# Layer 1 self attention of a Perceiver block: eight steps put in another order

## The chip, the cores and the metric

The kernel runs on one core of one Trainium2 chip. The metric is the time of one execution on the device in microseconds (us), as the median of several runs. Lower is better. All arithmetic is float32.

## What is computed

The reference is a two-layer Perceiver on 64 sequences of 32 tokens with 256 features. Each layer adds a cross attention, a self attention and a feed-forward part to `x`. The change lies in the last two parts of layer 1. In short, with `ln` the layer norm:

```python
# self attention: 16 heads of 16 features, 4 groups of keys and values
q = einsum('bse,hed->bhsd', ln(x), Wq) + bq
k, v = repeat(kg, 4), repeat(vg, 4)          # kg, vg: 4 groups, from ln(x)
scores = einsum('bhqd,bhkd->bhqk', q, k) / sqrt(d)      # causal mask
x = x + concat_heads(softmax(scores) @ v)
# experts: each token goes to the one expert with the highest router value
route = sigmoid(ln(x) @ router_w)            # 8 experts
e, p = argmax(route), max(route)
x = x + p * ((silu(ln(x) @ gate_w[e]) * (ln(x) @ up_w[e])) @ down_w[e])
```

## The kernel before

The 2048 tokens are 16 tiles of 128 rows (four sequences each), called `xs[0]` to `xs[15]`; they stay on the chip. Four tiles make a group, since a projection takes 512 columns at once. TensorE (PE), VectorE (DVE) and ScalarE (ACT) run exactly in the order in which the program is written: these stages are inside `manual_schedule` for the three. GpSimd (POOL) and the DMA queue of SyncE (SP) are ordered by the framework's planner.

**The attention loop.** `for t in range(NT - 3)` at the end of the kernel is a pipeline written out by hand. In turn t, PE computes the scores of tile t+1 (`score`), the result of tile t-1 (`gather`), the values of tile t+1 (`values`), and the turn of tile t's probabilities (`heads_on_partitions`, L286, copied by ACT in L288). Around them lie the pieces of other work:

- `softmax_rows` reads the scores on DVE (L268, L277), and POOL subtracts the maximum (L278). `power(t + 1)` takes the exponential on ACT (L2120).
- `place_values` copies the values of tile t+1 out of the PSUM bank "v" into a block form: one quarter on DVE (L2144), three on ACT (L2146). There is one bank "v", so `values` of the next tile waits until all four copies are done.
- `gather` ends with a reciprocal and a product on DVE (L2161, L2163) and an addition into `xs[t-1]` on POOL (L2166).
- `group(g, part)` prepares the next group of four tiles: part 0 turns the normalised tiles (`transposed_part`, PE L261, ACT L262) in two halves, both through the bank "mm"; parts 1 and 2 are the projections (L1476), copied by ACT.
- `bias` and `norm` (L1459, L205) prepare later groups; `load_piece` starts the loads of expert weights on SP.

**The router**, within the same loop. For a set of tiles (`ROUTED`: 0 to 3, then pairs): `route_stats` takes mean and variance on DVE (L179, L180), and after the set's last tile `route_scale` makes the norm's scale on POOL (L164 to L1840, eight small operations for a pair). `route_norm` applies it on ACT (L1849), `route_turn` turns it (PE L1865, ACT L1870), `route` multiplies with the router's weights (PE L1879) and takes an exponential on ACT (L1888). `choose_expert` finds the best expert on DVE (L1894 to L1904; POOL stores the weight in L1905). `places` ranks the tokens within each expert by matmuls with `oh` and `cum` (L1918, L1921; DVE L1925 to L1930). `send` writes each token's row to its place in a sorted array in memory by an indirect DMA on POOL (L1938). `heat` issues matmuls whose result nobody uses (L1909).

**After the loop** the last three tiles and the first expert tiles are written out turn by turn. The expert part works on 20 tiles of 128 sorted rows: `load_rows` (SP, L2217; it waits for all sends so far), `rows_norm` (DVE L2247), `rows_turn` (PE L2263, ACT L2265), `gate` and `up` (PE, L2307), `hidden_of` (ACT L2337, DVE L2338, L2339), `turn_hidden` (PE L2346, ACT L2351), `down` (PE L2307, DVE L2362, and an indirect DMA to the output on POOL, L2365). Tiles 0 to 2 may start once the first 10 token tiles are sent, tiles 3 and 4 after 12, the rest after all 16 (`give_count`, `give_table`). The banks "o", "mm", "PT" and "v" of PSUM are each there once; two uses of one bank follow each other.

Of the kernel before, what the change touches and what calls it, by code (L numbers as in the profile page):

```python
# [15 lines left out]
NT = B * S // P  # L16
# [23 lines left out]
def bc(ap, axis, n):  # L40

    shape = list(ap.shape)
    shape.insert(axis, n)
    return ap.unsqueeze(axis).to_broadcast(shape)
# [3 lines left out]
def perceiver_kernel(ctx: ExitStack, tc: tile.TileContext, a: dict, out: bass.AP):  # L48
# [209 lines left out]
    def transposed_part(xn, xT, ps, k, name, tag="mm"):  # L258
        tp = ps.tile([P, 512], F32, tag=tag, name=f"tp_{name}_{k}")
        for i in range(4):  # L260
            nc.tensor.transpose(tp[:, i * P : (i + 1) * P], xn[i][:, k * P : (k + 1) * P], ident)  # L261
        nc.scalar.copy(xT[:, k, :], tp)  # L262
# [18 lines left out]
    def heads_on_partitions(s, ps, t, work, name):  # L281

        pt = ps.tile([P, 512], F32, tag="PT", name=f"ptp_{name}{t}")
        sf = s.rearrange("p h k -> p (h k)")
        for c in range(4):
            nc.tensor.transpose(pt[:, c * P : (c + 1) * P], sf[:, c * P : (c + 1) * P], ident)  # L286
        pT = work.tile([P, 4, P], F32, tag="pT", name=f"pT_{name}{t}")
        nc.scalar.copy(pT.rearrange("p c q -> p (c q)"), pt)  # L288
        return pT
# [110 lines left out]
    with tc.tile_pool(name="wA", bufs=2) as work, tc.tile_pool(  # L400
# [77 lines left out]
        def power(t):  # L478
            nc.scalar.activation(sc[t], sc[t], AF.Exp)
# [39 lines left out]
        def gather(t):  # L519
            pT, vd = turned.pop(t), vals.pop(t)  # L520
            o_ps = ps1.tile([P, KC, P], F32, tag="o", name=f"oa{t}")
            for j in range(4):
                for c in range(4):
                    p0 = 64 * (c % 2)
                    nc.tensor.matmul(
                        o_ps[p0 : p0 + 64, c // 2, j * S : (j + 1) * S],
                        vd[:, j, c].rearrange("p h d -> p (h d)"),
                        pT[:, c, j * S : (j + 1) * S],
                        start=True,
                        stop=True,  # L530
                    )
            oT = ctxo[t] = work.tile([P, KC, P], F32, tag="oT", name=f"oTa{t}")
            nc.scalar.copy(oT, o_ps)


            if 2 <= t < 10:
                z, h4 = divmod(t - 2, 4)
                if z == 0:
                    dst = b_q[:, h4 // 2, (h4 % 2) * 1024 : (h4 % 2) * 1024 + 1024]
                    src = a["b_wq"].rearrange("(k p) o -> p k o", p=P)[  # L540
                        :, h4 // 2, (h4 % 2) * 1024 : (h4 % 2) * 1024 + 1024
                    ]
                    nc.gpsimd.tensor_copy(dst[:, 0:1], oT[:, 0, 0:1])
                else:
                    dst = b_o[:, 4 * h4 : 4 * h4 + 4, :]
                    src = a["b_wo"].rearrange("(h p) o -> p h o", p=P)[:, 4 * h4 : 4 * h4 + 4, :]
                    nc.gpsimd.tensor_copy(dst[:, 0, 0:1], oT[:, 0, 0:1])
                nc.sync.dma_start(dst, src)
# [338 lines left out]
    with tc.tile_pool(name="wB", bufs=2) as work, tc.tile_pool(  # L887
# [228 lines left out]
        ff, late = {}, []  # L1116
# [705 lines left out]
    def route_stats(t):  # L1822
        ts = next(ts for ts in ROUTED if t in ts)
        if t == ts[0]:
            rows[ts] = sm(f"lnf_{t}", [P, 4, 2])
        stats(rows[ts][:, t - ts[0], :], xs[t], f"f{t}")
        if t == ts[-1]:
            route_scale(ts)
# [43 lines left out]
    def route(ts, ps, tag):  # L1872

        n_, t0 = len(ts), ts[0]
        xT = rows.pop(ts)[1]
        l_ps = ps.tile([P, n_, NE], F32, tag=tag, name=f"lpf{t0}")
        for i in range(n_):
            for k in range(KC):
                nc.tensor.matmul(  # L1879
                    l_ps[:, i, :],  # L1880
                    xT[:, k, i * P : (i + 1) * P],
                    f_r[:, k, :],
                    start=(k == 0),
                    stop=(k == KC - 1),
                )
        rt = sm(f"rtf_{t0}", [P, n_, NE])

        nc.scalar.activation(rt, l_ps, AF.Exp, scale=-1.0)  # L1888
        return lambda: choose_expert(ts, rt)

    def choose_expert(ts, rt):

        n_, t0 = len(ts), ts[0]
        nc.vector.tensor_scalar_add(rt, rt, 1.0)  # L1894
        nc.vector.reciprocal(rt, rt)
        mx = sm(f"mxf_{t0}", [P, n_])
        nc.vector.tensor_reduce(mx, rt, AX.X, ALU.max)
        nc.vector.tensor_tensor(rt, rt, bc(mx, 2, NE), ALU.is_equal)
        nc.vector.tensor_tensor(rt, rt, bc(desc[:, 0:NE], 1, n_), ALU.mult)
        m2 = sm(f"m2f_{t0}", [P, n_])  # L1900
        nc.vector.tensor_reduce(m2, rt, AX.X, ALU.max)
        nc.vector.tensor_tensor(oh[:, t0 : t0 + n_, :], rt, bc(m2, 2, NE), ALU.is_equal)
        for i, t in enumerate(ts):
            nc.vector.tensor_add(cum[:, t + 1, :], cum[:, t, :], oh[:, t, :])  # L1904
            nc.gpsimd.tensor_scalar(xf[t][:, D + 1 : D + 2], mx[:, i : i + 1], 0.5, None, ALU.mult)  # L1905
# [172 lines left out]
    with tc.tile_pool(name="wE", bufs=2) as work, tc.tile_pool(  # L2078
# [14 lines left out]
        def group(g, part):  # L2093


            if g >= NG or part == 3:
                return []
            if part == 0:
                e_group_start(g)
                return [  # L2100
                    lambda k=k: transposed_part(lat[g], feats[g][2], ps2, k, f"e{g}")
                    for k in range(KC)
                ]
            return [lambda o=o: e_features(g, part, o, ps2) for o in range(KC)]
# [32 lines left out]
        def place_values(t, v_ps, rs_=range(4)):  # L2137

            for r in rs_:
                rs = slice(32 * r, 32 * r + 32)  # L2140
                dst = vd[t % 3][rs].rearrange("p j c h d -> p (j c) h d")[:, :, r, :NH]
                src = v_ps[rs].rearrange("p j (c d) -> p (j c) d", c=4)
                if r == 0:
                    nc.vector.tensor_copy(dst, src)  # L2144
                else:
                    nc.scalar.copy(dst, src)  # L2146
# [31 lines left out]
        def choose_now():  # L2178
            for fn in chosen:
                fn()  # L2180
            chosen.clear()
# [215 lines left out]
        for t in range(NT - 3):  # L2397


            at_ = t + (t > 2)  # L2400
            parts = group(at_ // 4 + 1, at_ % 4) if t > 1 else []
            parts += router_parts(t)
            if t > 0:
                score(t + 1, idle=int(t > 10))
            if t < 12:
                load_piece()
            if t in (6, 11):
                route_norm(steps_n[t], work)
            for t_ in sends.get(t, ())[:1]:
                send(t_)  # L2410
            for fn in parts[:1]:
                fn()
            if t > 0:
                gather(t - 1)
            if t < 12:
                load_piece()
            for t_ in sends.get(t, ())[1:]:
                send(t_)
            for fn in parts[1:2]:
                fn()  # L2420
            choose_now()
            if t in (8, 9):

                route_norm(steps_n[t], work)
            v_ps[t + 1] = values(t + 1)
            place_values(t + 1, v_ps[t + 1], (0,))
            for fn in parts[2:3]:
                fn()
            choose_now()
            turned[t] = heads_on_partitions(sc.pop(t), ps1, t, work, "e")  # L2430
            power(t + 1)
            late = t < NT - 5
            if not late:
                place_values(t + 1, v_ps.pop(t + 1), (1, 2, 3))
            for fn in parts[3:]:
                fn()
            if t in steps_n:
                route_turn(steps_n[t], work, ps2, ("o", "mm"))
            if late:
                place_values(t + 1, v_ps.pop(t + 1), (1, 2, 3))  # L2440
            norm((t + 1) // 4 + 2, (t + 1) % 4, "e", mvs, lat)
            if t % 4 in (0, 3) and 0 < (t + 1) // 4 < NG - 1:
                bias((t + 1) // 4 + 1, t % 4 == 0)
            if 0 < t:
                route_stats(t - 1)
            if 1 < t < 10:
                load_piece()
# [21 lines left out]
        route_stats(t - 1)  # L2469

        t = NT - 2
        chosen.append(route(p10, ps1, "mm"))
        norms_to(1)
        gather(t - 1)
        choose_now()
        give_done()
        norms_to(2)
# [46 lines left out]
        turn_rows_to(4, "mm")  # L2524
        turn_rows_to(5, "v")
        hidden_of(2)
        places(p14, ps1, "o")
        for t_ in p14:
            send(t_)
        give_count(NT, ps1, "PT")  # L2530
        down(1, "mm")
        turn_hidden(2, "v")
        give_table()
        loads_to(FIRST[2] + 4)
# [140 lines left out]
```

## Time and profile before

| what | value |
|---|---|
| median of 3 runs | 1144.27 us (1143.97 to 1146.88) |
| the profiled execution | 1134.37 us, of which 1132.3 us are the span from first to last instruction |
| PE busy | 1092.7 us (97% of the span) |
| DVE, ACT, POOL busy | 769.7, 572.8, 465.8 us (68%, 51%, 41%) |
| granted TensorE clock | 0.999 (mean) |
| attention of layer 1 | first scores at 899.2 us, last at 990.2 us |
| expert products | first at 997.4 us; from 1035.4 us on one tile takes 5.8 us of PE |

A busy share is a mean over the whole span: it tells which engine is short of time over all, not what a single wait costs. A timeline line gives start, duration, engine, source line, operation, output and inputs, count, and in brackets how long the engine was idle before it and what ended that idle time. In a table of waits the three numbers are the total in us, the number of times, and the longest. "issue" stands for idle time that no wait of the program explains.

### The profile page before, as it was taken

Reading aid. Unit: us, or ns where it says so; the run is one execution under the profiler, and the core shown is the slowest. Engines: PE = TensorE matmul, PEld = TensorE weight load, DVE = VectorE, ACT = ScalarE, POOL = GpSimd, SP = SyncE. Lnnn points to the kernel's source line nnn. Section 1 sums busy time; section 2 is a strip of 40 time slices with the busy share of each in tenths; the row PEclk is TensorE's granted clock in tenths of the full one; section 3 lists DMA queues with packets and bytes.
Section 4 is the critical chain, followed back from the end, with each engine's and each line's share of the span. In section 5 each row is a group of like instructions: output and inputs, shape, how many; then the busy total and the mean of one; then the engine's idle time right before and its main releaser. Section 6 shows DMA issues by size and latency. Waiting matters only on the chain. (4 is left out here: it accounts for less than half of the span.)

```text
span 1132.3 us, 26384 instructions
## 1 busy us (share of the span) xinstructions
PE 1092.7 (97%) x10024; PEld 779.8 (69%) x10024; DVE 769.7 (68%) x1804; ACT 572.8 (51%) x1436; POOL 465.8 (41%) x781
## 2 busy tenths in 40 slices
PE   8999999999999989999999999999999988889997
PEld 5667867777677646677776777777777656656653
DVE  6887167677988997764226787777878666775532
ACT  4446354455354465232237777777777456442221
POOL 2443438878678687510001121111222346742111
PEclk9999999999999999999999999999999999999999
DMA  6220143654444544690232121223230044312413
GB/s 155 65 91 22 33 127 116 175 160 121 127 128 130 176 136 143 215 251 19 76 75 32 29 57 30 75 57 85 57 84 20 1 118 130 107 40 71 157 42 118
DMA packets 98958, 109.05 MB, mean 96 GB/s; under 512 B 37208, under 2 KB 73433, under 8 KB 98610
## 3 DMA queue, kind: packets, MB, share of 16 engines
q1 hardware_dynamic: 96290, 102.92, 32.1%
q0 software_dynamic: 1728, 4.33, 1.1%
q8 instruction: 80, 1.31, 0.5%
q14 instruction: 44, 0.36, 0.1%
q10 hardware_dynamic: 816, 0.13, 0.1%
HBM read 76.36 MB, written 31.41 MB: 95 GB/s over the span
## 5 line engine op out<-in xcount | busy, mean ns | idle before, releaser
L1556 ACT ACTIVATE pp<-Sd,nm 128x256 f32<-128x256 f32 x256 | 119.6, 481 | 40.6 <-POOL nm L1553 40.6
L919 PEld LDWEIGHTS qb<-xT_b,b_q 128*128 128x128 f32 x512 | 94.7, 190 | 39.0 <-issue 19.0
L919 PE MATMUL qb<-xT_b,b_q 128*128 128x256 f32 x512 | 121.3, 385 | 0.0
L1553 POOL TENSOR_SCALAR nm<-nm 128x2 f32<-128x2 f32 x128 | 26.9, 210 | 219.1 <-DVE nm L1552 218.9
L1010 PE MATMUL yb<-b_o,oTb 128*128 128x256 f32 x512 | 113.5, 380 | 0.5 <-DVE oTb L1002 0.5
L1552 DVE TENSOR_REDUCE nm<-Sd 128x2 f32<-128x512 f32 x128 | 79.4, 682 | 49.1 <-PE Sd L1539 49.1
L1010 PEld LDWEIGHTS yb<-b_o,oTb 128*128 128x128 f32 x512 | 96.4, 190 | 14.4 <-issue 1.8
L1574 DVE TENSOR_TENSOR pp<-pp,rd 128x512 f32<-128x512 f32 x128 | 89.6, 700 | 4.4
L1590 ACT COPY pTd<-pt 128x512 f32<-128x512 f32 x128 | 68.8, 591 | 10.3 <-PE pt L1584 4.2
L927 ACT COPY qTb<-qb 128x512 f32<-128x512 f32 x64 | 37.4, 584 | 69.8 <-PE qb L919 65.8
L938 POOL TENSOR_TENSOR q2b<-qTb 128x512 f32<-128x512 f32 x64 | 64.7, 1041 | 14.6 <-ACT qTb L927 14.6
L1584 PE MATMUL pt<-cst,pp 128*128 128x128 f32 x512 | 67.8, 274 | 2.5 <-DVE pp L1574 1.3
L1584 PEld LDWEIGHTS pt<-cst,pp 128*128 128x128 f32 x512 | 59.1, 141 | 11.9 <-ACT ld L1564 2.1
L972 DVE RECIPROCAL rqb<-rqb 128x512 f32<-128x512 f32 x16 | 53.5, 3342 | 17.8 <-ACT rqb L967 17.8
L1343 PE MATMUL qd<-xT_d,d_m 128*128 128x256 f32 x256 | 62.6, 387 | 0.7 <-DVE rd L1573 0.3
L1631 PE MATMUL yd<-d_n,co 128*128 128x256 f32 x256 | 63.2, 391 | 0.0
L1565 POOL TENSOR_TENSOR sd<-sd,ld 128x2 f32<-128x2 f32 x128 | 26.3, 205 | 86.2 <-ACT ld L1564 86.2
L1539 PE MATMUL Sd<-ct,qTd 64*128 64x256 f32 x480 | 60.0, 388 | 0.0
L1605 PE MATMUL od<-pTd,na 128*64 128x256 f32 x480 | 58.4, 385 | 0.0
L773 PE MATMUL yc<-c,hc 128*128 128x256 f32 x256 | 58.4, 381 | 0.0
L1631 PEld LDWEIGHTS yd<-d_n,co 128*128 128x128 f32 x256 | 46.2, 189 | 16.7 <-DVE nm L1552 7.7
L986 DVE RECIPROCAL rdb<-denb 128x512 f32<-128x512 f32 x16 | 53.7, 3355 | 5.8 <-PE denb L984 5.6
(462 smaller groups left out, 2407.9 us busy)
## 6 DMA issues: line engine op xcount, KB each, us to landing
srt<-pad SPq DMA_DIRECT2D x17, 1040.0 KB
mb<-maskd SPq DMA_DIRECT2D x64, 128.0 KB
ct<-ctd SPq DMA_DIRECT2D x30, 257.0 KB
rct<-in_ctxT_dram SPq DMA_DIRECT2D x32, 128.5 KB
rrt<-in_ctxT_dram SPq DMA_DIRECT2D x64, 64.2 KB
ctd<-rct SPq DMA_DIRECT2D x32, 128.5 KB
nad<-rna SPq DMA_DIRECT2D x16, 256.0 KB
fg<-in_f_wg_dram SPq DMA_DIRECT2D x16, 256.0 KB
```

Source lines behind the costliest of these rows:

```text
L773: nc.tensor.matmul(y_ps, hs[f][:, i * P : (i + 1) * P], c_2[:, f, :], start=(f == 0), stop=(f == 7),)
L919: nc.tensor.matmul(q_ps[:, hh, :], b_q[:, k, h * P : (h + 1) * P], xT[:, k, c0 : c0 + 256], start=(k == 0), stop=(k == KC - 1),)
L938: nc.gpsimd.tensor_tensor(q2[:, 4 * h4 : 4 * h4 + 4, :], q, q, ALU.mult)
L1010: nc.tensor.matmul(y_ps, oT[:, h, :], b_o[:, h, :], start=(h == 0), stop=(h == NH - 1))
L1343: nc.tensor.matmul(q_ps[:, r, :], m[:, k, pr * P : (pr + 1) * P], xT[:, k, c0 : c0 + 256], start=(k == 0), stop=(k == KC - 1),)
L1539: nc.tensor.matmul(logits[b][hh][:, u, :], qT[hs, b % 8, 4 * u : 4 * u + 4, :], ct[hs, b % 4, :KEYS], start=True, stop=True,)
L1552: nc.vector.tensor_reduce(nm, s_ps[hh], AX.X, ALU.max, negate=True)
L1556: nc.scalar.activation(pb[:, u, hh, :], s_ps[hh][:, u, :], AF.Exp, bias=nm[:, u : u + 1], accum_out=sd[:, u : u + 1],)
L1574: nc.vector.tensor_tensor(pp, pp, bc(rd, 2, KEYS), ALU.mult)
L1584: nc.tensor.transpose(pts[c][:, hh * 256 + u * P : hh * 256 + u * P + P], probs[b][:, u, hh, c * P : (c + 1) * P], ident,)
L1590: nc.scalar.copy(pT[:, c, :], pt)
L1631: nc.tensor.matmul(y_ps, co[:, pr, :], n[:, pr, :], start=(pr == pr0), stop=(pr == pr0 + n_pr - 1),)
```

## The change

No instruction is added or removed. Eight places change their order or their bank:

1. and 2. In turns t = 0 and t = 5 ACT's three copies of the values of tile t+1 come ahead of the exponential `power(t + 1)` instead of behind it.
3. and 4. In the part 0 of groups 2 and 3 (turns t = 3 and t = 7) the second half of the turn goes through the bank "PT" instead of "mm".
5. In turn t = 10 the choice of the experts of tiles 6 and 7 comes behind the values of tile 11 and DVE's copy of them, and `route_stats(9)` (with its `route_scale` on POOL) moves from the end of the turn into the middle of that choice.
6. In turn t = 11 ACT's three copies of values come behind the router's turn instead of ahead of it (`late`).
7. In turn t = 14 the router's product of tiles 10 and 11 comes behind `gather(13)`.
8. In the last turn `down(1)` comes ahead of `places`, `send` and `give_count` of tiles 14 and 15, and the two exchange the banks "o" and "mm".

```diff
-        return lambda: choose_expert(ts, rt)
+        return lambda between=None: choose_expert(ts, rt, between)
 
-    def choose_expert(ts, rt):
+    def choose_expert(ts, rt, between=None):
...
         nc.vector.tensor_tensor(rt, rt, bc(mx, 2, NE), ALU.is_equal)
+        if between is not None:
+            between()
         nc.vector.tensor_tensor(rt, rt, bc(desc[:, 0:NE], 1, n_), ALU.mult)
...
                 return [
-                    lambda k=k: transposed_part(lat[g], feats[g][2], ps2, k, f"e{g}")
+                    lambda k=k: transposed_part(lat[g], feats[g][2], ps2, k, f"e{g}", ("mm", "PT")[k])
                     for k in range(KC)
                 ]
...
             for fn in parts[1:2]:
                 fn()
-            choose_now()
+            if t != 10:
+                choose_now()
...
             for fn in parts[2:3]:
                 fn()
+            if t == 10:
+                chosen.pop()(lambda: route_stats(t - 1))
             choose_now()
             turned[t] = heads_on_partitions(sc.pop(t), ps1, t, work, "e")
+            if t in (0, 5):
+                place_values(t + 1, v_ps.pop(t + 1), (1, 2, 3))
             power(t + 1)
-            late = t < NT - 5
-            if not late:
+            late = t < NT - 4
+            if t not in (0, 5) and not late:
                 place_values(t + 1, v_ps.pop(t + 1), (1, 2, 3))
             for fn in parts[3:]:
                 fn()
             if t in steps_n:
                 route_turn(steps_n[t], work, ps2, ("o", "mm"))
-            if late:
+            if t not in (0, 5) and late:
                 place_values(t + 1, v_ps.pop(t + 1), (1, 2, 3))
...
-            if 0 < t:
+            if 0 < t and t != 10:
                 route_stats(t - 1)
...
         t = NT - 2
-        chosen.append(route(p10, ps1, "mm"))
         norms_to(1)
         gather(t - 1)
+        chosen.append(route(p10, ps1, "mm"))
         choose_now()
...
         hidden_of(2)
-        places(p14, ps1, "o")
+        down(1, "o")
+        places(p14, ps1, "mm")
         for t_ in p14:
             send(t_)
         give_count(NT, ps1, "PT")
-        down(1, "mm")
         turn_hidden(2, "v")
```

## The prediction

> **What bounds the kernel now.** I read the page first, then the waits of PE over 899 to 1040 us (the self attention of layer 1, then the first expert tiles), then the timelines of the engines around each wait. The page gives one engine nearly all of the span:
>
> ```profile
> PE 1092.7 (97%) x10024; PEld 779.8 (69%) x10024; DVE 769.7 (68%) x1804; ACT 572.8 (51%) x1436; POOL 465.8 (41%) x781
> ```
>
> PE runs in written order and from 1035 us on is nearly without a gap, so whatever PE gains before that, the end gains too. The waits of PE in 899 to 1040 us (total, times, longest) say what there is to gain:
>
> ```profile
> PE ve L2128 <- ACT vde L2146: 5.0, 3, 2.4
> PE lpf L1879 <- ACT xTf L1870: 1.9, 3, 0.7
> PE tp_e L261 <- ACT xT_e L262: 1.6, 2, 1.1
> PE rank L1918 <- DVE oh L1902: 1.3, 1, 1.3
> PE S_e L311 <- issue: 1.3, 1, 1.3
> ```
>
> The edits aim at the first four rows: all of the first, third and fourth, and two of the second row's three waits (0.73 each): 5.0 + 1.6 + 1.3 + 1.5 = 9.4 us. That is the ceiling. The sum below asks at each place what is late next.
>
> **Steps 0 and 3 (copies of values ahead of the exponential; the second turn into bank PT).** The edit at t = 0 moves three copies of 1.15 us together (L2146) ahead of a 0.63 us exponential, so the 0.98 us wait of `values(2)` at 910.54 shrinks by 0.65. At t = 3 the second turn needs no copy out of the one bank "mm"; 1.07 us at 920.36 go, since "PT" is free once ACT has copied heads 2 (917.97). Together 1.7 us. Behind them stands this:
>
> ```profile
> 915.35 1.37 PE L2128 MATMUL ve<-e_v,xT_e 128*32 128x64 f32 x64
> ...
> 920.36 0.66 PE L261 MATMUL tp_e<-cst,xn_e 128*128 128x128 f32 x4 [1.07 <-ACT xT_e L262]
> ...
> 922.56 0.82 PE L311 MATMUL S_e<-kde,qTe 32*32 32x64 f32 x60
> 924.64 0.30 PE L311 MATMUL S_e<-kde,qTe 32*32 32x64 f32 x4 [1.25 <-issue]
> ```
>
> Sixty of 64 like matmuls run, PE stops for 1.25 us with nothing to wait for, and four follow; earlier a block of 64 that takes 1.10 us elsewhere took 1.37. The page has a queue for it:
>
> ```profile
> q8 instruction: 80, 1.31, 0.5%
> ```
>
> 80 packets for 20,048 matmuls and weight loads are about 250 instructions each. The DMA records show five of these packets between 904 and 925 us, at 905.97, 909.77, 913.87, 917.80 and 922.40: one every 3.8 to 4.6 us, near the shortest spacing of the whole stage (3.7). The stop at 924.64 ends 1.3 us after the last one's end (922.40 + 0.97). I read it as the supply of PE's instructions. [...] If the supply is already saturated nothing stays, if it isn't the limit all does; I take 0.85, the middle of 0 and 1.7.
>
> [...]
>
> **Steps 5 and 7 (copies ahead at t = 5, second turn of group 3).** PE waits 2.41 us at 939.84 for copies that stand behind an exponential, and that one stands behind POOL:
>
> ```profile
> 937.99 0.63 ACT L2120 ACTIVATE s_e<-s_e 128x512 f32<-128x512 f32 x1 [1.29 <-POOL s_e L278]
> 938.64 1.15 ACT L2146 COPY vde<-ve 32x256 f32<-32x256 f32 x3
> ```
>
> After: the copies run in ACT's idle 1.29 us (936.7 to 937.9), `values(7)` starts at 938.0 to 938.2, 1.7 us early. ACT still waits for POOL to 937.99, then runs four norms (L1849, 2.08): done at 940.7 instead of 941.9. Next comes the exponential of tile 7, which ran at 942.40. Its input is POOL's subtraction of 940.82 to 941.87, which hangs on DVE's 938.67 (itself a wait of 1.77 for POOL's x): this chain doesn't move. So the exponential runs at 941.92, 0.48 early, and with it the copies of xTf (L1870) that free "mm" at 944.05. The second turn into "PT" then takes away the 0.52 us wait at 945.83 whole. Gain 0.48 + 0.52 = 1.0; bounds 0.5 (the turn alone) and 2.9 (both waits whole).
>
> **Step 10 and 11 (choice behind the copy of values, rank statistics inside it; xTf's copy ahead of values').** Here DVE held back ACT's copies:
>
> ```profile
> 971.43 0.40 DVE L2144 COPY vde<-ve 32x256 f32<-32x256 f32 x1
> ...
> 978.31 0.43 DVE L179 BATCH_NORM_STATS2 lnb_f<-x 128x6 f32<-128x256 f32 x1 [1.71 <-POOL x L2166]
> ```
>
> The copy at 971.43 waited for the ten operations of the choice (968.09 to 971.5). Put first it runs at 968.1, ACT's copies at 969.7 to 970.85, and `values(12)` at 971.5 instead of 973.07. It costs DVE nothing: the choice's first operation took 0.56 us for 0.17 because POOL's subtraction ran to 968.63. The statistics inside the choice now wait for POOL's x (970.59); behind that wait stand the rest of the choice (0.9 us), the ranks of tiles 4 and 5 and the scores of tile 12. The two broadcast operations at 969.18 and 969.92 took 0.71 each beside POOL, so DVE was blocked until 970.63 anyway: scores of 12 again at about 972.75 (972.80). POOL's eight scale operations (2.3 us from L164) start at 971.8 instead of 972.96, ahead of the two L1905 (0.42). So POOL's subtraction of tile 12 starts at about 974.5 instead of 975.19, and DVE's 978.31 becomes 977.6.
>
> On PE, `values(12)` gains 1.6, and xTf's copy ahead of 1.15 us of value copies takes the 0.73 us at 978.97: 2.0 to 2.3 us early at 979. But at t = 12 PE needs `oh` of tiles 8 and 9 (rank at 983.91, behind four idle matmuls that hid the wait), and DVE makes that: 0.7 from POOL's x, and the 0.38 it waited for PE at 980.70, less what POOL's add (983.39, now 982.6) blocks. `oh` comes 0.85 to 0.9 early. Gain 0.9; bounds 0 (DVE takes the wait for POOL's x in full) and 2.3. A new PE wait of about 1.1 us for `oh` appears there.
>
> **Route behind the gather (t = 14).** The gather (0.71) covers the 0.73 us at 992.95, but then `values(15)` needs the bank that ACT's copies free at 994.58, and it started at 994.64. Gain 0.05; at most 0.7.
>
> **down(1) ahead of the last ranks.** PE idles 1.32 us at 1020.14. Now eight matmuls (1.81 apart) run there and the ranks come at 1020.5. Next, `turn_hidden(2)` needs DVE's product, ending at 1021.88: 0.73 early, not 1.32. DVE gets down's 0.48 us (L2362) ahead of the ranks, but loses it behind them, so the product of tile 3 still ends at 1027.62 and its turn starts at 1027.67 instead of 1028.26: 0.6. POOL gets one output transfer (1.0 us) ahead of two sends: the last send goes from 1024.67 to about 1025.1, lands 2.6 later, and the rows of tile 5, issued at 1027.35, come 0.5 late. Their user ran at 1032.93, their transfer takes about 2.3: 3 us of slack cover it. On SP nothing else moves. Gain 0.6; bounds 0.4 and 1.3.
>
> **Sum.** 0.85 + 1.0 + 0.9 + 0.05 + 0.6 = 3.4 us. The profiled execution took 1134.37 us (span 1132.3 and 2.1 around it), so 1131.0. The runs shown have a median 9.9 us above it, which no view places; I carry the difference over: **1140.9 us**.
>
> **Rivals.**
> 1. *The waits go whole.* POOL, DVE and the instruction supply give way: up to 9.4 us, 1134.9. Against it stand the rows above, each with its next waiter. [...] Chance 0.22.
> 2. *Given back.* The supply is saturated (first term 0) and DVE takes the new wait for POOL's x in full (third term 0): 1.65, 1142.6. POOL's order is a planner's, not written out; if it leaves the scale operations where they were, the same follows. For it: packets 3.8 us apart before any edit. Chance 0.13.
> 3. *Slower, by the clock.* New idle time of PE at the ranks of tiles 8 and 9. The granted clock is 1.00 over 899 to 990, a 2.41 us idle included; over 1126 to 1132, past the last matmul, its mean is 0.77. If the new wait there exceeds those 2.4 us, and the clock halves for one step of 7 us (980 to 987, PE busy 6.7), 6.7 us are added: 1147.6. It decides only when `oh` is 1.3 us later than worked out. Chance 0.05.
>
> [...]
>
> **How the numbers follow.** The sum has 0.60, spread about evenly over 1139.5 to 1142.3. A difference under 0.3% (3.4 us) is about what a measurement of this kernel can tell from none; that bound, 1140.8, cuts the sum's case in halves. Faster: 0.30 + 0.22 = 0.52. Slower: 0.04 of the clock's case. Same: the other 0.44. The range leaves out the clock and the larger half of rival 1, and adds rival 2 with some margin: 1138.0 to 1143.4.
>
> **What would show it.** Right: no PE wait for L2146 over 1 us; ACT at t = 5 still waiting for POOL's L278; the issue stop near 924 still there or larger; a wait of PE for `oh` near 982; rows of tile 5 not waited for. Wrong: PE at tile 3's first expert product (1023.09) more than 4.8 or less than 2 us early, or a clock under 1.00 in 899 to 1030.

## The result, and the profile after

| | before | after |
|---|---|---|
| median | 1143.88 us (1139.64 to 1146.88, 8 runs) | 1136.91 us (1136.21 to 1139.27, 8 runs) |
| the profiled execution | 1134.37 us, span 1132.3 | 1137.79 us, span 1135.8 |
| granted clock of the profiled execution | 0.999 | 0.996 |

The ratio of after to before on record is 0.9958, 95% interval 0.9941 to 0.9975: faster by 0.42%. (The plain quotient of the two medians would be 0.9939.) On the 1144.27 us that the prediction started from this is 1139.5 us, within its range; the median of 1136.91 itself lies 1.1 us below it. But the profiled execution of the faster kernel is 3.4 us slower than that of the slower one. So the two traces, laid side by side, say the opposite of the medians. This has to be explained before any single edit can be.

The waits of PE in 899 to 1040 us of the kernel after (total, times, longest):

```profile
PE S_e L311 <- issue: 3.5, 4, 2.1
PE ve L2130 <- ACT vde L2148: 1.6, 3, 0.6
PE tpf L1865 <- DVE fd L1426: 1.4, 1, 1.4
...
PE tph L2348 <- DVE hs L2341: 0.9, 1, 0.9
...
PE rank L1920 <- DVE oh L1904: 0.6, 1, 0.6
```

(Lines after L1889 stand one or two further down than before.) The waits that the edits aimed at are gone or short: 5.0 for the copies of values became 1.6, the 1.3 for `oh` ahead of the last ranks is gone (the 0.6 for `oh` here is a new wait, at 985.12), and the row of 1.6 for the second turn is no longer there (0.4 of it is left as a wait of `values(4)`, at 920.99). In their place the stops for which no wait accounts ("issue") grew from 1.3 to 3.5 in the scores alone.

**What differs between executions.** The trace also holds the clock granted to PE, and it changes in steps: it is 1.00 or 0.50, and each half-rate stretch in the stage lasts 3.41 us or, in two of the 14 profiles, 6.83. The kernel after has two in its profile. Here are the windows (start and end, length, then busy time of PE, PEld, DVE, ACT and POOL with counts, granted clock, share of the DMA engines, GB/s), cut to where the clock steps:

```profile
922.35:925.76 3.41, 1.28 (x68) 0.85 (x65) 1.74 (x8) 2.24 (x5) 0.24 (x1) 1.00 0.51 163
925.76:929.18 3.42, 3.42 (x8) 1.17 (x4) 1.39 (x3) 0.00 (x0) 1.05 (x1) 0.50 0.35 98
994.03:997.45 3.42, 2.66 (x81) 2.15 (x66) 2.23 (x6) 2.43 (x6) 1.78 (x2) 1.00 0.19 49
997.45:1000.86 3.41, 3.12 (x70) 2.55 (x62) 2.90 (x15) 0.63 (x2) 1.09 (x3) 0.50 0.29 78
```

In the first pair PE was busy for only 1.28 of 3.41 us, and the next window runs at half clock; the four projections in it take 3.65 us (L1476, at 925.79) where they took 1.98 in before (at 924.87). The starts of the two stretches lie 71.68 us apart, 21 times 3.413 (71.68 / 21). In the nine profiles with several stretches in the stage their distances are such whole multiples (before_again, below: 71.68 and 27.31, 21 and 8 times). So the steps of one profile lie on a grid of windows of 3.413 us, and executions of one program fall on it differently: the first stretch of the stage starts at 925.76 us here and 2.0 us later in after_again (927.76), where PE itself is 1.1 us later (scores of tile 5 at 923.69 instead of 922.61). The profiled execution of before has no such step before its last matmul; its clock is 1.00 up to 1129.2 us and 0.50 from there to the end of the span. Counted back from that step by 62 windows of 3.413 us, an estimate that takes the grid to hold so long, its windows fall like this:

```profile
917.58:920.99 3.41, 2.34 (x84) 1.74 (x78) 2.80 (x10) 2.65 (x6) 2.59 (x3) 1.00 0.61 160
920.99:924.41 3.42, 2.39 (x129) 1.93 (x129) 1.92 (x8) 2.24 (x5) 0.75 (x2) 1.00 0.47 158
924.41:927.82 3.41, 3.02 (x41) 1.52 (x41) 1.64 (x4) 1.27 (x3) 1.05 (x1) 1.00 0.36 97
...
938.06:941.47 3.41, 1.63 (x69) 1.43 (x70) 2.69 (x10) 3.34 (x8) 2.60 (x4) 1.00 0.24 72
```

The idle time around 920 and 924 us is shared out over three windows, and no window of the stage has less than 1.63 us of work. That was a rare case: of 105 later runs of the kernel before none had a mean clock above 0.997, and 87 were at 0.995 or less. The execution whose durations the prediction added up was, by clock, the best that this kernel was seen to have.

### The profile page after: what moved, and what is told of

Read it like the earlier page. It is cut to its first block, busy times and chain, and to the rows that moved or that the text cites. A ratio compares the mean times of both kernels' runs of the same rounds, so it can differ in the third digit from the quotient of the medians.

```text
span 1135.8 us, 26386 instructions
## 1 busy us (share of the span) xinstructions
PE 1096.3 (97%) x10024; PEld 781.9 (69%) x10024; DVE 770.8 (68%) x1804; ACT 573.2 (50%) x1436; POOL 467.3 (41%) x781
## 5 line engine op out<-in xcount | busy, mean ns | idle before, releaser
L1590 ACT COPY pTd<-pt 128x512 f32<-128x512 f32 x128 | 68.8, 591 | 10.1 <-PE pt L1584 4.3
```

The costliest lines, as they stand in the source:

```text
L1590: nc.scalar.copy(pT[:, c, :], pt)
```

## The experiments

Two theories. **Order**: the time fell because PE waits less; a part's gain is the idle time that it takes. **Clock**: the time fell because fewer windows are so empty that the next one runs at half rate; what counts is where the idle time lies and not how much there is. The second could be tested since `heat`, matmuls that nobody uses, puts work into a wait without moving anything else.

The twelve kernels ran in three sets on three chips, each set beside 35 runs of the kernel before on the same chip; the column "before" shows the set. "Lost" is the mean over the runs of (1 - granted clock) times the time; a stretch of 3.41 us at half rate counts 1.7. Over 248 runs, each kernel about its own mean, the time goes up by 0.77 us (0.71 to 0.82) per us lost (correlation 0.86). "By clock" is that slope times the difference in lost; "rest" is what is left of the difference of the means to before, uncertain by 0.5 to 0.9 (95%). The slope is, if anything, too low: lost also counts the half clock behind the last matmul, where nothing is left to slow down (1.5 us in the profile on record), and each clock is noted to 0.001, which is 1.1 us.

| kernel | median (before) | ratio, 95% interval | lost (before) | mean difference | by clock | rest |
|---|---|---|---|---|---|---|
| before_again | 1142.36 (1141.12) | 1.0011, 0.9994 to 1.0028 | 7.8 (7.8) | +0.8 | 0.0 | +0.8 |
| mid_only | 1140.34 (1141.12) | 0.9989, 0.9973 to 1.0004 | 6.0 (7.8) | -1.6 | -1.4 | -0.2 |
| choice_only | 1140.66 (1141.12) | 0.9992, 0.9980 to 1.0003 | 8.2 (7.8) | -1.1 | +0.3 | -1.4 |
| after_heat | 1137.92 (1141.12) | 0.9969, 0.9954 to 0.9985 | 4.1 (7.8) | -3.7 | -2.9 | -0.9 |
| after_again | 1135.90 (1139.45) | 0.9965, 0.9951 to 0.9980 | 4.4 (8.3) | -4.3 | -3.0 | -1.2 |
| early_only | 1137.91 (1139.45) | 0.9986, 0.9968 to 1.0005 | 6.4 (8.3) | -1.8 | -1.5 | -0.3 |
| down_only | 1137.09 (1139.45) | 0.9978, 0.9960 to 0.9995 | 5.1 (8.3) | -2.6 | -2.4 | -0.1 |
| before_heat_end | 1137.41 (1139.45) | 0.9983, 0.9965 to 1.0001 | 5.1 (8.3) | -2.3 | -2.4 | +0.1 |
| after_heat_14 | 1135.60 (1139.00) | 0.9967, 0.9950 to 0.9984 | 3.6 (7.3) | -3.5 | -2.8 | -0.7 |
| after_heat_both | 1134.94 (1139.00) | 0.9971, 0.9957 to 0.9985 | 2.7 (7.3) | -4.2 | -3.5 | -0.8 |
| before_heat_all | 1136.52 (1139.00) | 0.9979, 0.9962 to 0.9996 | 2.1 (7.3) | -2.2 | -4.0 | +1.8 |
| route_only | 1139.58 (1139.00) | 1.0014, 0.9994 to 1.0033 | 6.9 (7.3) | +1.2 | -0.3 | +1.5 |

One run of before_heat_all took 2810 us and is in its median but in none of its means. The rest of before_again, the same program built anew, is +0.8: a rest below about that size tells nothing by itself. The intervals of the ratio leave out 1 for the four kernels in the new order, for down_only and for before_heat_all; they include it for before_again, mid_only, choice_only, early_only, before_heat_end and route_only.

### The two kernels again: before_again, after_again

No edit in either.

> The kernel before, unchanged, to read the granted clock of each of its executions. Theory order (the gain is PE's saved waits): the clock of its executions is that of the changed kernel, 0.995 to 0.997, and the ratio to the kernel before is 1.000. Theory clock (most of the measured gain comes from fewer stretches at half clock): clocks of 0.993 or less in executions near 1144 us, 0.998 or more near 1134 us, about 2 us for each 0.0015 of clock.

> The changed kernel once more, beside the kernel before on this chip. Both theories: ratio 0.994 to 0.9975 as before. Theory clock: mean clock of its executions 0.995 to 0.997 against 0.993 of the kernel before, and about 2 us of the 4 to 5 us are the clock's.

The kernel before, profiled again, took 1140.41 us, 6.0 more than the profile on record, with three stretches at half clock. Its windows:

```profile
922.77:926.18 3.41, 1.88 (x67) 1.10 (x55) 2.08 (x9) 2.24 (x5) 0.00 (x0) 1.00 0.26 65
926.18:929.60 3.42, 3.42 (x36) 1.67 (x35) 1.01 (x4) 0.69 (x1) 1.05 (x1) 0.50 0.34 98
939.84:943.25 3.41, 1.74 (x70) 1.54 (x71) 2.81 (x11) 3.34 (x8) 2.60 (x4) 1.00 0.30 80
943.25:946.66 3.41, 2.85 (x100) 2.08 (x103) 3.31 (x9) 3.34 (x8) 3.24 (x6) 1.00 0.66 166
1021.76:1025.17 3.41, 2.09 (x19) 1.85 (x18) 1.97 (x10) 1.33 (x4) 2.35 (x4) 1.00 0.32 115
1025.17:1028.58 3.41, 3.41 (x10) 2.78 (x10) 2.72 (x13) 0.00 (x0) 0.90 (x1) 0.50 0.01 1
```

The same program, the same instructions: here the wait near 924 lies within one window, and the next one is slow. Laid against the profile on record, matmul by matmul, the stretches at 926, 998 and 1025 cost 1.3, 1.2 and 1.7 us (0.4 of the second comes back behind it). Longer stops for issue cost another 2.1: 0.3 at 924, 0.4 at 964 to 974 and 1.4 at 987 to 992. So 6.0 of the 9.9 us that no view had placed are seen here: not around the program and not spread over it, but in steps inside it, two thirds of them by the clock and one third where PE stops with nothing to wait for. The other 3.9 stand in no trace. A time like the median of 1144.27 goes with more stretches: the nine runs of before with a clock of 0.990 took 1143.9 us on the mean (over the three chips). The kernel after repeats its gain: ratio 0.9965 (0.9951 to 0.9980).

The third and fourth line of the fence are the counterexample: 1.74 us of work, and no step. Over the 14 profiles, in 895 to 1045 us, all nine windows with less than 1.5 us of PE work are followed by one at half clock, 7 of 15 with 1.6 to 2.2 us, and eight fuller ones too, with up to 3.04 us (windows that ran at half clock themselves aren't counted). So the busy time of PE alone does not sort the windows; what does was not shown.

### Where the order's gain went: idle time by cause

The waits of PE summed over 899 to 1035 us, from each profile:

| kernel | stops for issue | other waits |
|---|---|---|
| before; before_again; route_only | 1.3; 3.8; 1.1 | 13.8; 11.6; 13.5 |
| mid_only; choice_only; early_only; down_only | 4.2; 4.1; 3.7; 2.3 | 10.0; 10.1; 10.0; 11.3 |
| after; after_again | 5.1; 3.9 | 8.2; 8.9 |

From the first row to the last the other waits fall by 4.4 us on the mean (13.0 to 8.6), and the stops for issue rise by 2.4 (2.1 to 4.5). By these means about half of what the edits take away from the waits comes back where PE stops with nothing to wait for, and 2.0 us of order are left. But the kernel before alone lies between 1.3 and 3.8, so the size of that rise is not shown by three profiles against two. The 1.4 us at 987 to 992 come and go with the execution: before_again, mid_only, choice_only, after and after_heat have them, at the same scores, the other nine profiles don't.

One of the stops does go with the edits. It is the one in the scores of tile 5, near 924: 0.8 to 1.5 us in the seven profiles without the edits of steps 0 and 3, 2.1 to 2.4 in the four that have them (after, after_again, early_only, after_heat_14); the three with idle matmuls at this place are left out.

### The supply of instructions: after_heat

```diff
-                score(t + 1, idle=int(t > 10))
+                score(t + 1, idle=2 if t == 4 else int(t > 10))
```

on the kernel after: four idle matmuls of 512 columns (eight instructions with their weight loads) ahead of the scores of tile 5.

> The changed kernel with four idle matmuls of 0.5 us ahead of the scores of tile 5, where PE stopped for 2.1 us in the issue row and the clock then fell to half. Theory supply (PE waits for instructions there): the idle matmuls fit into the stop, which shrinks to under 0.5 us and now comes after 56 of the 64 score matmuls; the time is the changed kernel's or, if the clock holds there, about 2 us less. Theory without supply limit: 1.9 us more than the changed kernel.

In the kernel after PE stops behind 60 of the 64 score matmuls, as it did before, and for 2.12 us instead of 1.25:

```profile
922.61 0.82 PE L311 MATMUL S_e<-kde,qTe 32*32 32x64 f32 x60
925.56 0.30 PE L311 MATMUL S_e<-kde,qTe 32*32 32x64 f32 x4 [2.12 <-issue]
925.79 3.65 PE L1476 MATMUL qe<-xT_e,e_q 128*128 128x512 f32 x4
```

With the idle matmuls:

```profile
922.43 1.88 PE L1911 MATMUL S_e<-cst 128*128 128x512 f32 x4
924.25 0.79 PE L311 MATMUL S_e<-kde,qTe 32*32 32x64 f32 x56
925.20 0.31 PE L311 MATMUL S_e<-kde,qTe 32*32 32x64 f32 x8 [0.17 <-issue]
925.44 1.98 PE L1476 MATMUL qe<-xT_e,e_q 128*128 128x512 f32 x4
```

Eight instructions more, and the stop comes four matmuls (eight instructions) earlier in the program: it hangs on a count of instructions, not on a piece of data. Two other profiles have two idle matmuls there (before_heat_all, after_heat_both): the stop comes behind 58, after 1.23 and 1.28 us. And the matmul behind this stop starts 1.3 us after the end of a packet of q8 in the profile of before (at 924.64) and 1.2 us after one in that of after (at 925.56; the packet runs from 923.38 to 924.35). Together this is read as a stop for the supply of instructions; how many of them come at a time no run shows, beyond the mean of about 250 from 80 packets of q8 for some 20,000. The 1.88 us of idle matmuls cost nothing here: from the turn of the probabilities ahead of them to the projection it is 3.50 us (921.94 to 925.44) and without them 3.76 (922.03 to 925.79), and the projection runs at full clock. Yet the kernel as a whole gained nothing by it: its ratio is 0.9969, that of after_again 0.9965, and it lost 4.1 us of clock on the mean against 4.4 there. The profile with no stretch at all (1135.49 us) was one case of several. As a remedy the experiment missed; as a test of the stop it worked.

### Parts alone: early_only, mid_only, choice_only, route_only, down_only

early_only: the copies at t = 0 and the second turn of group 2.

```diff
+            if t in (0,):
+                place_values(t + 1, v_ps.pop(t + 1), (1, 2, 3))
             power(t + 1)
...
-                    lambda k=k: transposed_part(lat[g], feats[g][2], ps2, k, f"e{g}")
+                    lambda k=k: transposed_part(lat[g], feats[g][2], ps2, k, f"e{g}", ("mm", "PT")[k if g in (2,) else 0])
```

> Before, with the copies ahead of the exponential at t = 0 and the second turn of group 2 in bank PT. Theory supply: of the 1.7 us of waits 0.6 to 0.9 stay and the issue stop at 924 us grows from 1.3 to 2.1 us; with clock, this longer stop lets the half clock at 926 us come as often as before or more often: 0 to 0.9 us less. Without supply limit: 1.7 us less, stop of 1.3 us unchanged.

The stop for issue in its scores grew to 2.4 us, and the window that it lies in (923.17 to 926.58) has 1.01 us of work; a half-rate window follows. Its rest is -0.3. The time fell by 1.8 us on the mean. That is twice the most that the theory of supply allowed (0.9) and near the 1.7 written down without a limit of supply; but the stop grew, which only the first has, and 1.5 of the 1.8 go with the clock, where it expected no gain. The interval of the ratio includes 1, so the time decides nothing between them.

mid_only: the copies at t = 5 and the second turn of group 3 (the same diff with 5 and 3).

> Before, with the copies of values ahead of the exponential at t = 5 and the second turn of group 3 in bank PT, nothing else. Theory order: 1.0 us less than before (ratio 0.999), the 2.4 us wait of values(7) gone. Theory clock: that wait is the longest idle time of PE before, and without it the clock falls less often there: 2 to 4 us less in timed executions, with a higher mean clock.

The time is 1.6 us less on the mean, between the two theories, and its ratio can't be told from 1. Rest -0.2, with three half-rate stretches in its profile. The wait of `values(7)` went from 2.41 to 0.50, with a stop for issue of 0.34 behind it.

choice_only: the edits of t = 10 and 11 (5 and 6 in the list), as in the diff of the change.

> Before, with the choice of t = 10 behind the copy of values, the statistics inside it, and xTf's copy ahead of the values' copies at t = 11. Theory order: 0.3 to 0.9 us less. Theory clock: up to 2 us less, if the wait of values(12) (1.6 us) had a part in the half clock.

Rest -1.4, the only part whose rest is below zero by more than its uncertainty; its clock is no better than that of before. With a rest of +0.8 for the unchanged program in the same set, and a ratio whose interval includes 1, this is a hint that these edits save time by order, and not more.

route_only: edit 7 alone.

```diff
-        chosen.append(route(p10, ps1, "mm"))
         norms_to(1)
         gather(t - 1)
+        chosen.append(route(p10, ps1, "mm"))
```

> The kernel before with edit 7 alone (the router's product of tiles 10 and 11 behind the gather of tile 13). Theory order: 0.05 us, at most 0.7, ratio 0.999 to 1.001. Theory clock: the same, unless the one moved matmul changes the idle time ahead of the half clock at 997 us; then up to 1.7 us less, and the mean clock 0.0015 higher.

Same within the interval, as both theories said; its rest of +1.5 is beyond the 0.7 that they allowed, and nothing in its profile accounts for it but the stretches at half clock in the stage, two of 3.41 us and one of twice that. One of them follows a window with 1.00 us of work around the long wait of turn 5, another one a window with 2.68:

```profile
936.49:939.90 3.41, 1.00 (x63) 0.74 (x52) 1.57 (x6) 2.05 (x6) 3.33 (x5) 1.00 0.29 77
939.90:943.31 3.41, 3.41 (x73) 3.24 (x62) 3.00 (x9) 2.55 (x6) 2.31 (x3) 0.50 0.63 194
977.45:980.86 3.41, 2.68 (x90) 1.85 (x92) 1.81 (x5) 2.19 (x6) 2.46 (x3) 1.00 0.31 103
980.86:984.27 3.41, 3.41 (x101) 3.24 (x90) 2.55 (x11) 0.06 (x1) 2.79 (x4) 0.50 0.19 63
```

down_only: edit 8 alone.

```diff
-        places(p14, ps1, "o")
+        down(1, "o")
+        places(p14, ps1, "mm")
...
-        down(1, "mm")
```

> Before, with down(1) ahead of the last ranks alone. Theory order: 0.6 us less (ratio 0.9995). Theory clock: the half clock stretch that began at 1025 us in the profile of before_again is gone, mean clock up by about 0.0015, and 2 to 2.5 us less (ratio 0.998).

The largest part in time (-2.6 on the mean), and nearly all of it by clock: lost falls from 8.3 to 5.1, the rest is -0.1. But one stretch of 3.41 us counts 1.7, and the place behind the last ranks holds one in each execution at most. Of the 3.2 us less lost, 1.5 or more must lie at other places or be chance (the difference is uncertain by 1.7).

### Clock alone, in the old order: before_heat_end, before_heat_all

before_heat_end puts one `heat` ahead of the last ranks, into the wait that edit 8 fills with work:

```diff
-        places(p14, ps1, "o")
+        places(p14, ps1, "o", idle=1)
```

> Before, unchanged in order, with two idle matmuls (0.95 us together) in the 1.32 us wait ahead of the last ranks. Theory order: the same time as before (ratio 1.000), since the wait for oh stays. Theory clock: PE is busy in that window, the half clock at 1025 us is gone, 1.5 to 2 us less (ratio 0.998 to 0.9985).

Nothing is reordered, and the mean falls as in down_only: -2.3 and -2.6, lost 5.1 in both. The interval of its ratio just includes 1 (1.0001), and the limit of 1.7 us for one stretch holds here too, so this run alone is a hint and no proof. In before_again the wait of 1.32 us is followed by eight matmuls of `down(1)` at half rate:

```profile
1024.48 0.39 PE L1918 MATMUL rank<-oh,tri 128*128 128x16 f32 x2 [1.32 <-DVE m2f L1901]
...
1025.21 3.63 PE L2307 MATMUL ys<-fd,hs 128*128 x8
```

In the kernel after the same eight run ahead of the ranks, where the wait was, at full rate, and 0.91 us of wait for DVE's product come behind them:

```profile
1022.04 1.89 PE L2309 MATMUL ys<-fd,hs 128*128 x8
1023.76 0.29 PE L1920 MATMUL rank<-oh,tri 128*128 128x16 f32 x2
...
1025.40 0.63 PE L2348 MATMUL tph<-cst,hs 128*128 128x128 f32 x4 [0.91 <-DVE hs L2341]
```

before_heat_all puts idle matmuls at five places of the old order, none of the eight edits. Each `heat` of 1 is two matmuls in the trace, so the six of the expectation are twelve (and one is two in after_heat_14):

```diff
-                score(t + 1, idle=int(t > 10))
+                score(t + 1, idle=1 if t == 4 else int(t > 10))
...
+            if t in (6, 11):
+                heat(ps1.tile([P, 512], F32, tag="PT", name=f"idle{t}"), 2 if t == 6 else 1)
...
+        heat(ps1.tile([P, 512], F32, tag="PT", name="idle14"), 1)
...
-        places(p14, ps1, "o")
+        places(p14, ps1, "o", idle=1)
```

> The kernel before in its own order, with idle matmuls at the five places where profiles of the old order or of single parts show a stretch at half clock just behind (turns 4, 6, 11, 14 and ahead of the last ranks; six idle matmuls in all). None of the eight edits is in it. Theory clock: most of what the change gains is the granted clock, so the clock rises from 0.993 to 0.997 or more and the time falls 3 to 5 us below before, to about the time of the kernel after (1135 to 1138). Theory order: the gain of the change comes from the order alone, so this one takes the time of before, 1140 to 1141, or a little more.

Lost falls to 2.1, less than in any kernel of the new order, and the time by 0.21% (0.04% to 0.38%), 2.2 us on the mean. That goes against the order theory, which had no gain at all here. But it is less than the 3 to 5 us that the clock theory wrote down: the clock's 4.0 come with a rest of +1.8. Its trace shows that price: against the profile on record PE falls back by 1.1 us at the idle matmuls of turn 4, where the stop behind them did not shrink, and by 1.0 at those of turn 14; the other three places cost nothing.

### The new order with idle matmuls: after_heat_14, after_heat_both

after_heat_14 adds one `heat` ahead of the values of tile 15, after_heat_both another one ahead of the scores of tile 5 (`idle=1 if t == 4`):

```diff
+        heat(ps1.tile([P, 512], F32, tag="PT", name="idle14"), 1)
```

> The kernel after with one idle matmul (heat, bank PT) ahead of the values of tile 15 in turn 14, where the profile of the kernel after runs a stretch at half clock (997.4 to 1000.8 us). Theory clock: PE is idle for a good part of 992 to 997 there, and one matmul of about 0.4 to 0.5 us that nobody uses, lying in a wait that is there anyway, keeps the clock up: mean granted clock 0.997 to 0.998 instead of 0.996, time 1 to 2 us less than the kernel after in the same call or an earlier one (1134 to 1135.9). Theory order: only the order of the work counts, an idle matmul saves nothing: same as the kernel after or up to 0.5 us more (1135.9 to 1136.9), clock as before at 0.996.

> The kernel after with two idle spots filled: one idle matmul ahead of the last scores of turn 4 (behind which the stretch at half clock at 925.8 us lies) and one ahead of the values of tile 15 (997.4 us). Theory clock: both stretches go in nearly all executions, mean clock 0.9975 or more, 1 to 3 us less than the kernel after (1133 to 1135); before is 1140 to 1141 in the same call. Theory order: same as the kernel after, 1135.9 to 1137.

after_heat_14 did not do what it was for: its profile still has a half-rate stretch at 995.8 us, behind a window with 3.04 us of work. after_heat_both has the least lost clock of the new order (2.7) and the lowest median (1134.94), with the ratio 0.9971 (0.9957 to 0.9985). That is no better than the ratio of after_again, so no version is shown to beat the kernel after.

## Why the prediction was right, and where it was wrong

The direction and the size came out (predicted 3.4 us, measured 4.3 on the mean in after_again), but not by the sum; that the number fell into the range is luck. Of the 4.3, some 3.0 went with the clock, for which the sum had no term, and 1.2 are left for the order, for which it had 3.4. The four kernels in the new order have rests of -0.7 to -1.2, mean -0.9. (The split leans on the slope of 0.77; at 1.0 the order would keep 0.3 in after_again and nothing in the other three, which carry idle matmuls.) The text's own test says the same: tile 3's first expert product should have come 2 to 4.8 us early, and in the profile after it came at 1026.22, 3.1 late, with the clock under 1.00 in the stage.

The traces give the order's share without that slope. Take the start of one and the same matmul in a profile and in the profile on record, and see how the difference changes over a part of the stage that holds no half-rate stretch in the profiles named (positive: PE got ahead, in us; the times are those of the profile on record):

| edits, part of the stage | predicted | after_again | after | others with these edits |
|---|---|---|---|---|
| steps 0 and 3, 899.2 to 924.6 | 0.85 | -0.4 | -0.2 | early_only, after_heat_14: -0.4 |
| steps 5 and 7, 936.0 to 949.8 | 1.0 | 1.1 | 1.1 | mid_only, after_heat, after_heat_14, after_heat_both: 1.1 |
| steps 10 and 11, 958.0 to 986.1 | 0.9 | 0.65 | 0.3 | after_heat_14, after_heat_both: 0.65; choice_only, after_heat: 0.3 |
| route, 986.1 to 994.6 | 0.05 | 0.0 | -1.4 | |
| down(1), 1013.0 to 1041.3 | 0.6 | -0.1 | -0.1 | down_only, after_heat, after_heat_both: -0.1 |

The 0.3 and the -1.4 stand where stops for issue lie, and before_again, with no edit, falls back by 0.4 and 1.4 in the same two parts. In the first part the profiles without the edits of steps 0 and 3 and without idle matmuls there lie between -0.3 and +0.7, so the small minus is not told from nothing, but 0.85 is not reached by any with the edits. In after_again the column adds up to 1.2 us, a third of the sum. At full clock throughout, the profile of before has a span of 1132.3 us, and the two of the new order without a stretch ahead of the last matmul have 1131.0 (after_heat_both) and 1133.4 (after_heat, with the stops at 987 to 992); both carry four idle matmuls.

- **The base.** "which no view places; I carry the difference over" is the step that failed. What can be seen of the 9.9 us (6.0, in before_again) was two thirds half-rate windows and one third stops for issue, and it was not a constant to carry: the lost clock is smaller with the edits. The granted clock of the profiled execution, 0.999, was there to be read, but only one execution was, and no window of its stage had less than 1.63 us of PE work.
- **Steps 0 and 3** (0.85). The stop was there and larger, the gain was not: nothing stayed. A new stop of 0.64 us at 913.30 takes the gain of step 0. Up to the stop near 924 PE is 0.64 ahead, but that stop grows from 1.25 to 2.12 us, and behind it PE is no longer ahead but 0.2 to 0.4 late in all four profiles with these edits and no idle matmuls there. No run shows a supply of instructions that leaves 0.6 to 0.9 us of the 1.7, or the 0.85 of the sum; what the runs show in its place is a stop of 2.1 to 2.4 us that takes the whole gain. The grown stop also makes its window thin (1.28 of 3.41 us busy), and the slow window behind it costs another 1.4 to 1.7.
- **Steps 5 and 7** (1.0). This term came out, and it is the only one that did: PE gains 1.1 in all six profiles that have these edits. The copies fill ACT's wait, the exponential behind them does not move (937.99 before, 940.57 after, with PE 2.58 late on entry), and what is late next is the router's turn (1.41 for what the turn needs); the gain comes behind it, at the two turns of group 3, as worked out:

```profile
939.31 1.15 ACT L2148 COPY vde<-ve 32x256 f32<-32x256 f32 x3
940.57 0.63 ACT L2122 ACTIVATE s_e<-s_e 128x512 f32<-128x512 f32 x1
```

```profile
940.51 1.52 PE L2130 MATMUL ve<-e_v,xT_e 128*32 128x64 f32 x64 [0.50 <-ACT vde L2148]
...
944.02 1.06 PE L1865 MATMUL tpf<-cst,xn_f 128*128 128x128 f32 x8 [1.41 <-DVE fd L1426]
```

- **Steps 10 and 11** (0.9). PE kept 0.65 to 0.7 of it against profiles with the same stops for issue. The clause that failed is that POOL's scale operations come "ahead of the two L1905": the planner left those two where they were, in front (now L1907), so the scale starts 0.3 early and not 1.2. DVE's wait for POOL's x stayed, 1.82 us instead of 1.71. The new wait of PE for `oh` came, 0.64 us where 1.1 was worked out. On POOL, then on DVE:

```profile
973.63 0.43 POOL L1907 TENSOR_SCALAR x<-mxf 128x1 f32<-128x1 f32 x2
974.15 0.24 POOL L164 TENSOR_SCALAR lnr_f<-lnf 128x2 f32<-128x2 f32 x1
```

```profile
979.52 0.43 DVE L179 BATCH_NORM_STATS2 lnb_f<-x 128x6 f32<-128x256 f32 x1 [1.82 <-POOL x L2168]
```

- **Route** (0.05). Too small to see in time, as expected, and 0.0 in the trace.
- **down(1)** (0.6). The new wait is the one named, `turn_hidden(2)` for DVE's product, 0.91 us. In the trace it brings 0.65 at that turn, 0.15 to 0.3 at tile 3's first product and nothing from 1031 on, with stops for issue of 0.2 to 0.3 us behind the turn; in time nothing measurable by order (rest -0.1). What down_only gained went with the clock, for which there was no term: 2.4 us by the slope, 1.7 at most at this one place.
- **Rival 1** (waits go whole) fell: of the sum's five terms none came out clearly larger than worked out. **Rival 2** (given back, 1.65) is nearest to what the order did, 1.2: the grown stop took the first term whole, the planner part of the third, and the clock hid it. **Rival 3** named the clock, but with the sign and the condition wrong: it asked for a new idle time of more than 2.4 us in one piece and a step of 7 us. Stretches follow windows in which PE worked for 1.0 to 3.0 of 3.41 us, one lasts 3.41 us (6.83 in two of the 14 profiles), and the kernels in the new order lost less by them.
- Two small readings in the prediction were off and change no term: the choice has nine operations on DVE in the trace, not ten, and the scale for a pair seven on POOL, not eight.

## What to carry to other kernels

Before a sum is made on one profile, compare its granted clock and time with the median: here they differed by 9.9 us, that difference was a term of the kernel, and the change moved it. Where PE is the bound, look at each wait within the windows in which the clock stepped here, 3.41 us long: the wait of 1.32 us ahead of the last ranks lay in a window with 2.09 us of work in before_again, and the half rate behind it cost 1.7 us more. Filling such waits helped even without a change of order: idle matmuls at five places took 2.2 us off the mean (before_heat_all, ratio 0.9979, 0.9962 to 0.9996). Taking waits out ahead of a dense run of small matmuls brought nothing here: the stop in that run grew from 1.25 to 2.12 us; the edits behind it were the ones that still counted.

## What the runs showed of the hardware

- The clock granted to PE was 1.00 or 0.50, and its steps in one profile lie whole multiples of 3.413 us apart (71.68 and 27.31 in before_again); the kernel after has its first half-rate stretch of the stage at 925.76 us in one profile and at 927.76 in the other (after, after_again).
- The same program ran with a mean granted clock between 0.985 and 0.997 in 105 runs, and its time went with it (mean 1143.9 us for nine runs at 0.990, 1136.7 for twelve at 0.996, over three chips). It is not the edits alone that set it: these 105 runs have none of them.
- In the stage, over 14 profiles, the nine windows with less than 1.5 of 3.41 us of PE work were all followed by half rate, 7 of the 15 with 1.6 to 2.2 us, and eight fuller ones with up to 3.04 us, which busy time does not explain.
- The same matmuls at half rate: four projections 3.65 us (after) instead of 1.98 (before, after_heat), eight products of `down` 3.63 (before_again) instead of 1.89 (after).
- A stop of PE with nothing to wait for moved by two and four matmuls when two and four were put ahead of it (58 and 56 of 64 scores ahead of it instead of 60), and ended 1.3 and 1.2 us after a packet of the instruction queue in the profiles of before and after. With 2.12 us of stop and 1.28 of work in its window (after), it was followed by a half-rate window.
